# A graph convolution and a graph attention layer in fp32: one weight kept on chip, four reloaded through two buffers, norms moved, operands laid out anew

## The chip, the core and the metric

The kernel runs on one core of a Trainium2 chip. The core has five engines with a queue of instructions each: TensorE (PE in the profile, with PEld for its weight loads), VectorE (DVE), ScalarE (ACT), GpSimd (POOL) and SyncE (SP), which here issues every DMA. Engines wait for each other by semaphores; each works through its own queue in order. The metric is the device time of one execution in microseconds (us), as the median of several runs. Beside it there is one profiled execution, from which all durations here come.

## What is computed

The input is 128 graphs of 128 nodes with 512 features each, in fp32, and one adjacency matrix of 128x128. Two layers follow each other, both with a layer norm and a ReLU ahead and a residual addition behind:

```python
# layer 0: graph convolution
h = maximum(layernorm(x), 0)
norm_adj = adj * rsqrt(deg)[:, None] * rsqrt(deg)[None, :]
x = x + norm_adj @ (h @ weight) + bias
# layer 1: attention with 8 heads of 64, masked by adj
h = maximum(layernorm(x), 0)
q, k, v = h @ Wq + bq, h @ Wk + bk, h @ Wv + bv
scores = q @ k.T / 8 + (1 - adj) * -1e9
x = x + (softmax(scores) @ v) @ Wo + bo
```

All weights are 512x512. So each graph passes through five projections (W for the convolution, Q, K, V and the output), and the mixing by the adjacency matrix, the scores, the softmax and its product with v lie between them.

## The kernel before

**Groups and blocks.** Four graphs make a group, so there are 32 groups (`NG`). The main loop runs over t from 0 to 32, and a turn of it has five blocks, W, Q, K, V and Y, one for each projection. W(t) works on group t+1, Q, K and V on group t, Y on group t-1. A block has seven steps, W0 to W6 for instance, and each step a second part (W0b). `block` goes through the steps; at each it first calls what a dictionary called `plan` holds for this place, and then the step of the projection (`Projection.step` for the part without a letter, `rest` for b). `at(t, place, f, ...)` puts a call into the plan. This fixes the order of the instructions on every engine by hand; no scheduler moves them. SyncE has no steps of its own: a DMA is issued as soon as those before it in the queue are issued and its own semaphores allow.

**One projection.** A projection multiplies 512x512 by 512x512 blocks by the Winograd form of Strassen's method: seven products P1, P5, P2, P6, P3, P7, P4 of 256x256 blocks instead of eight, and three of these (P5 with P3, P2, P4) again in seven products of 128x128. The left operand (activations) and the right one (weights) are first combined: sums and differences of blocks, kept beside the blocks themselves. A full operand has 40 slots of 128 columns (128x5120 fp32, 2.6 MB). Left operands are combined for every group, by L367 to L370 (256-blocks) and by nine instructions of L78 (128-blocks), mostly on POOL. Weights are combined once, stored to DRAM with their sums and reloaded for every group.

PE's products go to PSUM banks: bank_a for the 256-products, bank_d (two banks) for P5 and P3, bank_b for P2, bank_c for P4. Step 1 writes bank_d with P5; VectorE adds it to the result in two parts (`read_seven`, L432), the second at step 2b. Step 2 writes the first phase of bank_b; step 4 its second phase and then P3 into bank_d again, for which VectorE must have left bank_d. P4's phases go to bank_c at step 6 and, as a `tail`, in steps 1 and 2 of the next block; K alone does them in its own steps 4 to 6 (`whole`).

**Weights.** Three buffers `w_buf` take the five weights in turn (order 0, q, k, v, o). `prefetch` issues a reload in four parts of ten slots, each at a step of the block that is running (steps 3 to 6; in Y all four at step 3). `keep_w` stores a combined weight to DRAM once.

**Norms.** `Norm.scale` does, for two graphs of a half group, BATCH_NORM_STATS (L320) and its aggregate (L321) of each, then `ve` (L322: variance plus epsilon) on VectorE, then the power (L323) and two small products (L325) on POOL. `ln1` calls it for the first layer at Q1b and Q3b, `ln2` for the second at V0 and V1b. ScalarE then writes the normalised graph (L336). Of the first layer it goes through PE for the mixing (`gcn_mix`, L604), of the second through PE for a transpose (`transpose_h`, L668), and ScalarE copies the result into the slots of the left operand (`blocks_of`).

**Attention.** At V0 stand `attend` of the group before (softmax times v, L797), the `scores` (L730, evicted by L737 or L734) and the combinations of the output operand. `row_max` (L749), `exponentials` (L757) and `softmax_end` (L764, L765) are spread over V, Y, and the next W and Q. For the transpose of the softmax, `split_att` (L770, L771) writes two planes of 16 bits to DRAM and `turn_att` (L774) reads them back by a transposing DMA.

Of the kernel before, what the change touches and what calls it, by code (L numbers as in the profile page):

```python
# [11 lines left out]
ALU = mybir.AluOpType  # L12
# [14 lines left out]
A11, A12, S1, A22, S2, S3, S4 = range(7)  # L27
# [16 lines left out]

LEFT_AT = {A11: 0, A12: 4, S1: 11, A22: 18, S2: 25, S3: 29, S4: 33}
RIGHT_AT = {W11: 0, T1: 4, W21: 11, T2: 18, W22: 22, T3: 29, T4: 33}
SLOTS = 40


# [20 lines left out]

def twice(t, at, n):

    return t[:, at[0] + n : at[1] + n + 1 : at[1] - at[0], :]


def combine_one(engine, t, at, step):
    out, x, y, minus = step
    engine.tensor_tensor(twice(t, at, out), twice(t, at, x), twice(t, at, y), ALU.subtract if minus else ALU.add)  # L78


def combine_within(engine, t, at, steps):
    for step in steps:
        combine_one(engine, t, at, step)


@with_exitstack
def kernel(
# [67 lines left out]


    w_sb, w_dram = {}, {}

    w_buf = [wp.tile([P, SLOTS, P], F32, tag=f"w{i}", name=f"w{i}") for i in range(3)]

    class Weight:
# [6 lines left out]
        def slot(self, k, n):  # L168
            return self.t[:, RIGHT_AT[k] + n, :]

# [9 lines left out]
    def keep_w(name):  # L180
        w_dram[name] = dp.tile([P, SLOTS, P], F32, tag=f"w_{name}", name=f"wd_{name}")
        nc.sync.dma_start(w_dram[name], w_sb[name].t)

    reloads = []

    def next_buffer():
        reloads.append(None)
        return w_buf[(len(reloads) - 1) % 3]

    def reload_w(name, part, parts):  # L190

        if part == 0:
            w_sb[name] = Weight(next_buffer())
        some = slice(part * SLOTS // parts, (part + 1) * SLOTS // parts)
        nc.sync.dma_start(w_sb[name].t[:, some, :], w_dram[name][:, some, :])

# [79 lines left out]
    def combine_inner(name, engine, steps=range(9)):  # L276
        for k in steps:
            pair, step = INNER[k]
            combine_one(engine, w_sb[name].t, tuple(RIGHT_AT[b] for b in pair), step)

# [25 lines left out]
    class Norm:  # L306


        def __init__(self, src, name):
# [5 lines left out]
            self.nb = sp.tile([P, 2], F32, tag="nb", name=f"nb_{name}")  # L315

        def scale(self, js):
            c = slice(js[0], js[-1] + 1)
            for j in js:
                nc.vector.bn_stats(self.st[:, j, :], self.src[:, j, :])  # L320
                nc.vector.bn_aggr(self.mv[:, j, :], self.st[:, j, :])  # L321
            nc.vector.tensor_scalar(self.ve[:, c], self.mv[:, c, 1], EPS, None, ALU.add)  # L322
            nc.gpsimd.tensor_tensor(self.rs[:, c], self.ve[:, c], mhalf[:, c], ALU.pow)  # L323
            for j in js:
                nc.gpsimd.tensor_scalar(  # L325
                    self.nb[:, j : j + 1], self.mv[:, j, 0:1], self.rs[:, j : j + 1], -1.0, ALU.mult, ALU.mult
                )
# [18 lines left out]
    class Operands:  # L346
# [6 lines left out]
        def slot(self, i, n):  # L353
            return self.t[:, LEFT_AT[i] + n, :]

        def blocks_of(self, b):

            half, j = divmod(b, 2)
            x, y = ((A11, A12), (S1, A22))[half]
            step = LEFT_AT[y] - LEFT_AT[x]  # L360
            t = self.t[:, LEFT_AT[x] : LEFT_AT[x] + 2 * step, :].rearrange("p (y s) n -> p y s n", y=2)
            return t[:, :, j : j + 3 : 2, :]

        def combine(self, engine, inner=True, then=None, within=None):

            t, then, within = self.blocks, then or engine, within or engine
            engine.tensor_tensor(t(S3), t(A11), t(S1), ALU.subtract)  # L367
            engine.tensor_tensor(t(S1), t(S1), t(A22), ALU.add)
            then.tensor_tensor(t(S2), t(S1), t(A11), ALU.subtract)
            then.tensor_tensor(t(S4), t(A12), t(S2), ALU.subtract)  # L370
            if inner:
                combine_within(within, self.t, (LEFT_AT[S1], LEFT_AT[S4]), FIRST_LEFT)
                combine_within(within, self.t, (LEFT_AT[A12], LEFT_AT[A22]), WINOGRAD_LEFT)

# [212 lines left out]

    def ln1(g, half, js=(0, 1)):
        if (g, half) not in scale1:
            scale1[g, half] = Norm(xts[g, half], f"1_{g}_{half}")  # L590
        scale1[g, half].scale(js)

# [4 lines left out]
    def gcn_mix(g, b):  # L597
        if b == 0:

            op_a[g] = op_att if g == 1 else op_mix  # L600
        h = hs.pop((g, b))
        pa = small_bank(f"pa_{g}_{b}")
        for c in range(NC):
            nc.tensor.matmul(pa[:, c * P : (c + 1) * P], h[:, c * P : (c + 1) * P], ant, start=True, stop=True)  # L604
        src = pa.rearrange("p (y c n) -> p y c n", y=2, c=2)
        if g == 1 and b < 2:
            nc.vector.tensor_copy(op_a[g].blocks_of(b), src)
        else:
            nc.scalar.copy(op_a[g].blocks_of(b), src)  # L609
# [42 lines left out]

    def ln2(g, half, js=(0, 1)):
        if (g, half) not in scale2:
            scale2[g, half] = Norm(xts[g, half], f"2_{g}_{half}")
        scale2[g, half].scale(js)

# [4 lines left out]
    def transpose_h(g, b):  # L662
        if b == 0:
            op_h[g] = op_norm
        h2 = hs.pop((g, b))
        pt = small_bank(f"pt_{g}_{b}")
        for c in range(NC):
            nc.tensor.transpose(pt[:, c * P : (c + 1) * P], h2[:, c * P : (c + 1) * P], ident)  # L668
        nc.scalar.copy(op_h[g].blocks_of(b), pt.rearrange("p (y c n) -> p y c n", y=2, c=2))

# [114 lines left out]
    def attend(g, b):  # L785
        if g not in op_o:

            op_o[g] = op_mix if g == NG - 1 else op_att
        aT = att_of(g, b if g == NG - 1 else b - 1)
        if b == 2 or b == 3:  # L790
            po = small_bank(f"po_{g}_{b}")
        else:
            po = bank["b" if b == 0 else f"a{1 - turn[0]}"]
        for c in range(NC):
            for p in range(2):
                h = 2 * c + p
                nc.tensor.matmul(  # L797
                    po[p * HD : (p + 1) * HD, c * P : (c + 1) * P],
                    vs[g][:, b, h * HD : (h + 1) * HD],
                    aT[:, p * NC + c, :],  # L800
                    start=True,
                    stop=True,
                )
        nc.scalar.copy(op_o[g].blocks_of(b), po.rearrange("p (y c n) -> p y c n", y=2, c=2))

# [19 lines left out]
    for t in range(-1, NG + 1):  # L825
# [3 lines left out]
        if 0 <= t - 1 < NG - 1:  # L829
            g = t - 1  # L830
            for place, first, f, *args in (
                ("W1", "W1", turn_att, 0),
                ("W1b", "W4b", split_att, 1),
# [4 lines left out]
                ("W6", "Q2", exponentials, 3, H // 2, H),  # L838
                ("Q0", "Q0", turn_att, 1),
                ("Q0b", "Q2b", softmax_end, 3),  # L840
                ("Q3b", "Q4b", split_att, 2),
                ("Q5b", "Q6b", split_att, 3),
                ("K1", "K1", turn_att, 2),
                ("K3", "K3", turn_att, 3),
            ):
# [18 lines left out]
        elif 1 <= t + 1 < NG and t >= 0:  # L864
            g = t + 1

            at(t, "V0", ln2, g, 0)
            at(t, "V1b", ln2, g, 1)
            at(t, "V5b", norm_h, g, 0)
            at(t, "V6", norm_h, g, 1)  # L870
# [12 lines left out]
        if 3 <= t + 2 < NG:  # L883
            at(t, "W3" if t > 1 else "W0", load_x, t + 2, (0,))
            at(t, "W6" if t > 1 else "W0", load_x, t + 2, (1,))
        if 2 <= t + 2 < NG:
            g = t + 2
            at(t, "Q0b" if t == 0 else "Q1b", ln1, g, 0)
            at(t, "Q3b", ln1, g, 1)
# [7 lines left out]
        if 0 <= t < NG:  # L897
# [16 lines left out]
            else:  # L914
                if t > 0:
                    at(t, "V4b", row_max, g, 1)
                    at(t, "Y1", exponentials, g, 1, 0, H // 2)
# [31 lines left out]


    uses = ["v", "o"]
    for t in range(2, NG + 1):
        uses += ["0"] if t + 1 < NG else []
        uses += ["q", "k", "v"] if t < NG else []
        uses += ["o" if t < NG else "o last"]

    def prefetch(part):
        if not uses:
            return
        if uses[0] != "o last":  # L960
            reload_w(uses[0], part, 4)
        elif part == 0:
            load_w("o last", wo, next_buffer())
        if part == 3:
            uses.pop(0)

    def block(t, kind, g, dense_of):
        dense = dense_of(g) if 0 <= g < NG else None
        for n in range(7):
            for place, part in ((f"{kind}{n}", 0), (f"{kind}{n}b", 1), (f"{kind}{n}c", 2)):  # L970
                for f, *args in plan.get((t, place), ()):
                    f(*args)
                if dense is not None and part < len(dense[n]):
                    if n > 2 and part == 0 and t > 0 and (t, kind) != (1, "W"):
                        for m in ((n - 3,) if kind != "Y" else range(4) if n == 3 else ()):
                            prefetch(m)
                    dense[n][part]()

    def prologue():
# [68 lines left out]
        at(0, "V0", combine_inner, "k", nc.gpsimd)  # L1048
        at(0, "V2", keep_w, "k")
        at(1, "Q2b", combine_w, "o", nc.gpsimd)  # L1050
# [6 lines left out]
    with tc.manual_schedule(  # L1057
# [7 lines left out]
    ):  # L1065
        prologue()

        for t in range(NG + 1):
# [52 lines left out]
```

## Time and profile before

| | |
|---|---|
| median of 3 runs | 2340.53 us (2339.39 to 2341.41) |
| the profiled execution, its own time | 2341.13 us |
| its span from the first to the last instruction | 2339.3 us |
| mean granted TensorE clock | 0.997 |
| period of one group in the middle of the run | 71.5 us |
| bytes moved by DMA | 617.35 MB, mean 264 GB/s, queue busy for 82.7% of 16 engines |

How to read the lines: a row of a timeline has the start in us from the span's start, the duration in us, the engine, the line of the kernel, the operation, the tile that it writes and those that it reads with shapes, and how many equal instructions are merged in the row. In brackets stands how long the engine was idle before it and what released it. A row of a waits view has who waited, for whom, the total in us, how often, and the longest. PE's matmuls are pipelined: a 128x128 one takes about 0.275 us from start to end, and the next starts 0.11 us after it.

### The profile page before, as it was taken

How to read it: one execution, taken by the hardware profiler on the slowest of the kernel's cores; microseconds unless marked ns; L12 is line 12 of the kernel's file. 1: busy time of each engine (PE TensorE's matmuls, PEld its weight loads, DVE VectorE, ACT ScalarE, POOL GpSimd, SP SyncE). 2: the span in 40 equal slices, each digit the busy share in tenths (PEclk: the TensorE clock that was granted, in tenths of full speed). 3: DMA queues.
4: the chain of work that ended last, by engine and by line, in shares of the span. 5: the costliest groups of instructions: out<-in, count | busy, mean ns of one | idle time of the engine just before them, and what ended most of it. 6: DMA issues, size and time to landing. Idle time of an engine off the chain costs nothing.

```text
span 2339.3 us, 51019 instructions
## 1 busy us (share of the span) xinstructions
PE 2291.9 (98%) x18359; PEld 2149.0 (92%) x18359; DVE 1881.7 (80%) x4832; ACT 1347.5 (58%) x3553; POOL 1862.7 (80%) x1927
## 2 busy tenths in 40 slices
PE   9889999999999999999999999999999999999999
PEld 8789999999999999999999999999999999999988
DVE  7767888788888878887888888788878888887876
ACT  3545656556656556565566565565655665655564
POOL 6888788777888777887778887778877788877664
PEclk9999999999999999999999999999999999999999
DMA  5488887898888998889988789987899888898773
GB/s 199 172 285 289 247 264 262 284 300 262 269 262 258 298 291 250 266 261 284 300 254 279 259 258 296 286 261 266 259 284 300 257 271 264 257 295 299 232 263 114
DMA packets 408189, 617.35 MB, mean 264 GB/s; under 512 B 273792, under 2 KB 281088, under 8 KB 407296
## 3 DMA queue, kind: packets, MB, share of 16 engines
q1 hardware_dynamic: 407936, 614.09, 82.7%
q8 instruction: 146, 2.39, 0.4%
q14 instruction: 107, 0.88, 0.1%
HBM read 437.33 MB, written 111.67 MB: 235 GB/s over the span
## 4 chain that ended last, share of the span: by engine, by line
PE 77%; DVE 14%; issue 2%; POOL 0%; ACT 0%; DVEq 0%
PE bank_a L391 27%; PE bank_d L391 17%; PE bank_c L391 10%; PE bank_b L391 7%; PE pa L604 4%; DVE st L320 3%; DVE v L432 3%; DVE q L432 3%; PE po L797 3%; DVE att L737 2%; PE pt L668 2%; PE bank_d L730 2%; DVE xt L432 1%; PE pss L730 1%; PE bank_b L797 1%
## 5 line engine op out<-in xcount | busy, mean ns | idle before, releaser
L757 ACT ACTIVATE att<-att,nmx 128x128 f32<-128x128 f32 x1024 | 396.0, 389 | 0.6 <-DVE nmx L749 0.5
L391 PE MATMUL bank_a<-op_h,w 128*128 128x256 f32 x1536 | 363.3, 379 | 0.0
L391 PEld LDWEIGHTS bank_a<-op_h,w 128*128 128x128 f32 x1536 | 277.6, 190 | 30.0
L765 POOL TENSOR_TENSOR att<-att,rsm 128x1024 f32<-128x1024 f32 x128 | 242.9, 1898 | 73.2 <-DVE rsm L764 69.9
L432 DVE TENSOR_TENSOR xt<-xt,bank_d 128x512 f32<-128x512 f32 x732 | 269.0, 416 | 27.0 <-PE bank_d L391 9.0
L336 ACT ACTIVATE h<-xt,nb,rs 128x512 f32<-128x512 f32 x254 | 204.0, 816 | 72.9 <-POOL nb L325 71.2
L691 ACT ACTIVATE q<-bank_a,bqk 128x256 f32<-128x256 f32 x192 | 80.5, 470 | 277.4 <-PE bank_a L391 277.4
L770 ACT COPY att<-att 128x2048 uint16<-128x2048 uint16 x124 | 235.5, 1899 | 8.1 <-POOL att L765 8.1
L391 PE MATMUL bank_d<-op_h,w 128*128 128x128 f32 (+1 forms) x1768 | 225.5, 279 | 11.1 <-DVE q L432 7.9
L391 PEld LDWEIGHTS bank_d<-op_h,w 128*128 128x128 f32 x1768 | 210.6, 192 | 17.2 <-issue 12.5
L78 POOL TENSOR_TENSOR op_o<-op_o 128x256 f32<-128x256 f32 x297 | 209.6, 729 | 10.0
L78 POOL TENSOR_TENSOR op_h<-op_h 128x256 f32<-128x256 f32 x279 | 197.0, 730 | 12.8 <-DVE op_h L370 3.2
L78 POOL TENSOR_TENSOR op_a<-op_a 128x256 f32<-128x256 f32 x270 | 190.9, 731 | 14.4 <-DVE op_a L370 5.1
L367 POOL TENSOR_TENSOR op_a<-op_a 128x512 f32<-128x512 f32 x29 | 37.0, 1275 | 203.6 <-ACT op_a L609 203.6
L757 ACT ACTIVATION_READ_ACCUMULATOR att<-att,nmx 128x1 f32 x1024 | 193.0, 188 | 0.0
L442 DVE TENSOR_TENSOR xt<-bank_a,xt 128x512 f32<-128x512 f32 x252 | 167.4, 685 | 18.5 <-PE bank_a L391 10.9
L391 PE MATMUL bank_a<-w,op_o 128*128 128x256 f32 x768 | 181.7, 379 | 0.0
L391 PE MATMUL bank_a<-w,op_h 128*128 128x256 f32 x744 | 179.1, 384 | 0.0
L391 PE MATMUL bank_a<-w,op_a 128*128 128x256 f32 x744 | 176.2, 380 | 1.2 <-DVE xt L442 1.2
L320 DVE BATCH_NORM_STATS2 st<-xt 128x6 f32<-128x512 f32 x256 | 172.3, 673 | 3.4 <-DMA xt<-in_x_dram 3.4
L705 ACT COPY v<-bank_a 128x512 f32<-128x512 f32 x96 | 56.3, 586 | 189.8 <-PE bank_a L391 145.4
L323 POOL TENSOR_TENSOR rs<-ve,mhalf 128x2 f32<-128x2 f32 (+1 forms) x129 | 92.1, 714 | 92.0 <-DVE ve L322 91.8
(178 smaller groups left out, 6091.9 us busy)
## 6 DMA issues: line engine op xcount, KB each, us to landing
w<-wd_v SPq DMA_DIRECT2D x124, 640.0 KB, 6.5
w<-wd_o SPq DMA_DIRECT2D x124, 640.0 KB, 6.9
w<-wd_q SPq DMA_DIRECT2D x120, 640.0 KB, 4.4
w<-wd_k SPq DMA_DIRECT2D x120, 640.0 KB, 8.0
w<-wd SPq DMA_DIRECT2D x116, 640.0 KB, 11.1
planes<-att SPq DMA_DIRECT2D x124, 512.0 KB, 4.4
xt<-in_x_dram SPq DMA_DIRECT2D x63, 512.0 KB, 6.7
out_dram<-xt SPq DMA_DIRECT2D x62, 512.0 KB, 3.9
```

The source lines that it names most:

```text
L78: engine.tensor_tensor(twice(t, at, out), twice(t, at, x), twice(t, at, y), ALU.subtract if minus else ALU.add)
L320: nc.vector.bn_stats(self.st[:, j, :], self.src[:, j, :])
L323: nc.gpsimd.tensor_tensor(self.rs[:, c], self.ve[:, c], mhalf[:, c], ALU.pow)
L336: nc.scalar.activation(h, src[:, j, :], AF.Relu, bias=nb[:, j : j + 1], scale=rs[:, j : j + 1])
L391: nc.tensor.matmul(out, lhsT, rhs, start=start, stop=True, skip_group_check=True)
L432: nc.vector.tensor_tensor(dst, dst, src, f)
L442: nc.vector.tensor_tensor(t, src.rearrange("p (r f) -> p r f", r=2), t, ALU.add)
L604: nc.tensor.matmul(pa[:, c * P : (c + 1) * P], h[:, c * P : (c + 1) * P], ant, start=True, stop=True)
L757: nc.scalar.activation(att[:, h, :], att[:, h, :], AF.Exp, bias=nmx[:, h : h + 1], scale=1.0, accum_out=sm[:, h : h + 1])
L765: nc.gpsimd.tensor_tensor(att, att, rsm.unsqueeze(2).to_broadcast([P, H, P]), ALU.mult)
L770: nc.scalar.copy(planes, halves)
L797: nc.tensor.matmul(po[p * HD : (p + 1) * HD, c * P : (c + 1) * P], vs[g][:, b, h * HD : (h + 1) * HD], aT[:, p * NC + c, :], start=True, s ...
```

## The change

Five things change; the order of PE's instructions does not.

- Weights: "k" stays in the third buffer for the whole run, and is neither stored nor reloaded. The other four ("0", q, v, o) share the first two buffers in turn, and are reloaded in four parts of 11, 11, 11 and 7 slots, cut where the products cut them (`PARTS`), at places listed by hand in `reloads_of`.
- Layer norm: the statistics of one graph (`statistics`) are a call of their own, so that `ln1` can do the first graph of a half at Q0b and the second, with the scale of both, at Q1b.
- The second norm's `ln2` goes from V0 and V1b to K0b and K3b; the first normalisation behind it from V5b to V5, and the second `row_max` of V from V4b to V3b.
- The transposing reads `turn_att` go from W1, Q0, K1, K3 to Q0, Q2, K0, K2; one x load goes from W6 to W5.
- The left operand's slots: the four plain blocks lie side by side (0, 4, 8, 12), the sums of 128-blocks behind them, so that `blocks_of` is one access with one stride. `twice` finds the slots by `slot_of`.

```diff
-LEFT_AT = {A11: 0, A12: 4, S1: 11, A22: 18, S2: 25, S3: 29, S4: 33}
+LEFT_AT = {A11: 0, A12: 4, S1: 8, A22: 12, S2: 16, S3: 20, S4: 24}
+LEFT_MORE = {A12: 28, A22: 31, S1: 34, S4: 37}
 RIGHT_AT = {W11: 0, T1: 4, W21: 11, T2: 18, W22: 22, T3: 29, T4: 33}
+PARTS = ((0, 11), (22, 33), (11, 22), (33, 40))
+def slot_of(left, k, n):
+    if not left:
+        return RIGHT_AT[k] + n
+    return LEFT_AT[k] + n if n < 4 else LEFT_MORE[k] + n - 4
...
         def blocks_of(self, b):
             half, j = divmod(b, 2)
-            x, y = ((A11, A12), (S1, A22))[half]
...
+            first = LEFT_AT[S1 if half else A11]
+            return self.t[:, first + j : first + 8 : 2, :]
...
+        def statistics(self, j):
+            nc.vector.bn_stats(self.st[:, j, :], self.src[:, j, :])
+            nc.vector.bn_aggr(self.mv[:, j, :], self.st[:, j, :])
         def scale(self, js):
             c = slice(js[0], js[-1] + 1)
-            for j in js:
-                nc.vector.bn_stats(self.st[:, j, :], self.src[:, j, :])
-                nc.vector.bn_aggr(self.mv[:, j, :], self.st[:, j, :])
             nc.vector.tensor_scalar(self.ve[:, c], self.mv[:, c, 1], EPS, None, ALU.add)
...
+        for j in js:
+            scale1[g, half].statistics(j)
+        if ready is None or ready:
+            scale1[g, half].scale(ready or js)
...
-                ("W1", "W1", turn_att, 0),
+                ("Q0", "W1", turn_att, 0),
...
-                ("Q0", "Q0", turn_att, 1),
+                ("Q2", "Q0", turn_att, 1),
...
-                ("K1", "K1", turn_att, 2),
-                ("K3", "K3", turn_att, 3),
+                ("K0", "K1", turn_att, 2),
+                ("K2", "K3", turn_att, 3),
...
-            at(t, "V0", ln2, g, 0)
-            at(t, "V1b", ln2, g, 1)
-            at(t, "V5b", norm_h, g, 0)
+            at(t, "K0b", ln2, g, 0)
+            at(t, "K3b", ln2, g, 1)
+            at(t, "V5", norm_h, g, 0)
...
-            at(t, "W6" if t > 1 else "W0", load_x, t + 2, (1,))
+            at(t, "W5" if t > 1 else "W0", load_x, t + 2, (1,))
...
-            at(t, "Q0b" if t == 0 else "Q1b", ln1, g, 0)
+            at(t, "Q0b", ln1, g, 0, (0,), ())
+            at(t, "Q1b", ln1, g, 0, (1,), (0, 1))
...
-                    at(t, "V4b", row_max, g, 1)
+                    at(t, "V3b", row_max, g, 1)
...
+    uses, reading = [], [-1]
+    for t in range(1, NG + 1):
         uses += ["0"] if t + 1 < NG else []
-        uses += ["q", "k", "v"] if t < NG else []
+        uses += ["q", "v"] if t < NG else []
         uses += ["o" if t < NG else "o last"]
+    def reload_w(n, part):
...
+        if part == 0:
+            w_sb[name] = Weight(w_buf[n % 2])
+        some = slice(*PARTS[part])
+        nc.sync.dma_start(w_sb[name].t[:, some, :], w_dram[name][:, some, :])
+    def reloads_of(t):
+        when = {
+            "W": ((t, "W6"), (t, "Q4"), (t, "Q1"), (t, "K3")),
+            "Q": ((t, "K4"), (t, "K6"), (t, "V0"), (t, "V1")),
+            "V": ((t, "V3"), (t, "Y0"), (t, "Y1"), (t, "Y3")),
+            "Y": ((t, "Y5"), (t + 1, "W0"), (t + 1, "W0"), (t + 1, "W3" if t + 1 < NG - 1 else "Q5")),
+        }
...
+        for kind in "WQVY":
...
+            reading[0] += 1
+            for part, place in enumerate(when[kind]):
+                at(*place, reload_w, reading[0] + 2, part)
...
-        at(0, "V2", keep_w, "k")
```

In `reloads_of`, the entry under "W" tells where the buffer that W reads is filled again, for V; that under "Q" the same for Y, under "V" for the next W, under "Y" for the next Q.

## The prediction

> **What bounds the kernel now.** I read the page's first part, then TensorE's own waits, then one steady group in order of time. The page:
>
> ```profile
> span 2339.3 us, 51019 instructions
> PE 2291.9 (98%) x18359; PEld 2149.0 (92%) x18359; DVE 1881.7 (80%) x4832; ACT 1347.5 (58%) x3553; POOL 1862.7 (80%) x1927
> ...
> w<-wd_k SPq DMA_DIRECT2D x120, 640.0 KB, 8.0
> ```
>
> PE is busy for 98%, so only its pauses can be won, and its matmuls are not touched: their order is the same in both kernels. The waits of PE alone say which pauses come back in every group (columns: total us, times, longest):
>
> ```profile
> PE bank_d L391 <- DVE v L432: 10.8, 28, 0.4
> PE bank_d L391 <- DVE q L432: 7.9, 29, 0.4
> ```
>
> Everything else in that view happens once or twice, at the ends. No matmul waits for a weight. In the group from 1000 to 1071.5 us (the period is 71.5 us) PE's two pauses stand here:
>
> ```profile
> 1024.67 0.61 PE L391 MATMUL bank_b<-w,op_h 128*128 128x128 f32 x4
> 1025.65 1.80 PE L391 MATMUL bank_d<-w,op_h 128*128 128x128 f32 x14 [0.38 <-DVE v L432]
> ...
> 1061.61 0.61 PE L391 MATMUL bank_b<-op_h,w 128*128 128x128 f32 x4
> 1062.48 1.80 PE L391 MATMUL bank_d<-op_h,w 128*128 128x128 f32 x14 [0.27 <-DVE q L432]
> ```
>
> Four 128x128 matmuls go out in 0.447 us, so bank_d was due at 1025.12 and came 0.54 late; its 14 matmuls then take 1.80 instead of 1.73. One V4 costs 0.61 us, one Q4 0.43 + 0.07 = 0.50. What makes VectorE late in V is here:
>
> ```profile
> 1020.02 0.68 DVE L320 BATCH_NORM_STATS2 st<-xt 128x6 f32<-128x512 f32 x1
> ...
> 1021.75 0.47 DVE L322 TENSOR_SCALAR ve<-mv 128x2 f32<-128x2 f32 x1
> ...
> 1023.59 0.86 DVE L432 TENSOR_TENSOR v<-v,bank_b 128x256 f32<-128x256 f32 x2
> 1024.37 1.14 DVE L432 TENSOR_TENSOR v<-v,bank_d 128x128 f32<-128x128 f32 x4
> ```
>
> VectorE does not rest from 1020.02 until it frees bank_d at 1025.51; the norm's 2.1 us stand in front. The trace holds its own control: the last group's V has no norm in it, and there PE goes
>
> ```profile
> 2298.01 0.61 PE L391 MATMUL bank_b<-w,op_h 128*128 128x128 f32 x4
> 2298.56 1.80 PE L391 MATMUL bank_d<-w,op_h 128*128 128x128 f32 x14
> ```
>
> that is 0.10 + 0.07 = 0.18 us, no more. The last Q (no norm either) shows the same 0.18 (2267.13 to 2267.68, then 1.80). This residue stays: bank_b's matmuls end late enough that VectorE's six additions (1.93 us) reach bank_d's release only 0.03 us before PE wants it.
>
> **The change, part by part.**
>
> *Second norm out of V (ln2 from V0, V1b to K0b, K3b).* V1b loses 2.1 us of VectorE. Its reads then start when bank_b is ready: PE's phase ends 1023.10, plus 1.93 is 1025.06, 0.05 before need. I take the control: 0.61 falls to 0.18, 0.43 x 30 groups = 12.9 us. The half at V0 lay in idle time (1.22 us stood before the first score eviction) and gains nothing there. row_max moving from V4b to V3b stays in front of the same six reads; ScalarE's normalisation at V5 instead of V5b fills a 1.4 us gap in which ScalarE waits for VectorE anyhow. Both: 0. On POOL, `rs` and `nb` of the norm (L323, L325: 0.7 + 0.5 us) move too: the first half's to a stretch of 7.28 us in which POOL waits for op_a, the second half's behind op_a's combinations at 1015.6, where the first half's stood; op_o's combinations behind them start when they did. 0.
>
> *First norm split (Q0b one element, Q1b the other).* In Q, VectorE stood idle 0.77 us before the bank_c read at 1057.40. One element's statistics (0.69 + 0.18, next instruction 0.82 later) fit in it to within 0.05. The rest at Q1b ends near 1058.95 instead of 1059.74; the bank_d and bank_c reads follow by 1059.81, and bank_b is ready at 1060.08, so again 1060.08 + 1.93 = 1062.01 against a need at 1062.05. 0.50 falls to 0.18: 0.32 x 29 = 9.4 us. Cover: the x load must have landed by 1056.5; before it landed at 1054.30 and was wanted at 1057.93.
>
> *What the norm costs in K.* K0b: VectorE idles 2.19 us before the bank_c read at 1000.52 and POOL is idle until 1003.64; 1.81 us fit. Cost 0. K3b is tight:
>
> ```profile
> 1006.27 0.61 DVE L432 TENSOR_TENSOR k<-k,bank_b 128x128 f32<-128x128 f32 x2 [0.24 <-PE bank_b L391]
> 1007.93 0.29 DVE L432 TENSOR_TENSOR k<-k,bank_c 128x128 f32<-128x128 f32 x1 [1.05 <-ACT k L694]
> ...
> 1008.52 0.61 PE L391 MATMUL bank_c<-op_h,w 128*128 128x128 f32 x4
> ```
>
> The norm now stands in front of these rows: VectorE's last bank_d addition starts at 1005.616, the next instruction 0.33 later, at 1005.95. It takes 1.81 (its length in Q, POOL idle: 1057.93 to 1059.74); behind it wait two bank_b additions (next start 0.53 later) and the bank_c addition (0.29), which K5's first bank_c matmul waits for. It frees bank_c at 1008.59; PE wants it at 1008.52. The nearest row for such a near miss is W's bank_c behind VectorE: released 0.008 us late it loses 0.153, so 0.065 + 0.145 = 0.21 us. Later steps of K keep their distance (bank_c's last phase is freed 0.1 before PE needs it). Bounds: 0 (VectorE a tenth faster) and 1.35 (below). 0.21 x 30 = 6.3 us.
>
> *Where row and rule part.* The norm's last instruction, `ve`, takes 0.17 us when POOL is idle (66 cases), but 0.46 to 0.50 in V under POOL's L370: in all of these it ended 0.023 us after POOL's instruction did. The Trainium skill (SBUF — State Buffer, "Who interferes with whom") speaks against the move: VectorE's tensor_scalar in its two-port mode and a GpSimd instruction share a port pair, and the one that issues first keeps it for its whole instruction. At K3b POOL combines op_a:
>
> ```profile
> 1006.35 1.27 POOL L369 TENSOR_TENSOR op_a<-op_a 128x512 f32<-128x512 f32 x1
> 1007.69 1.27 POOL L370 TENSOR_TENSOR op_a<-op_a 128x512 f32<-128x512 f32 x1
> ```
>
> `ve` is due at 1005.947 + 1.735 (from the first statistics to `ve`, as in Q) = 1007.68: over the steady groups 4 to 25 ns before L370 starts, inside a 67 ns gap. By the V row (0.3 held) K5 loses 0.51 and the sum is 7 us won. By the rule with `ve` first it is not held: 16 us won. With POOL first it is held till 1008.98, 1.14 us more: K5 loses 1.35. I take "first by start", but the stamps need not be the moment of asking: at 75.49 us VectorE's L296 took 1.30 us though the POOL instruction that held it started 22 ns after it.
>
> *K resident, four weights in two buffers.* Removes 120 DMAs of 640 KB (78.6 MB) and one 2.6 MB store: 617 to 536 MB. PE never waited for weights, so 0 is won. What it adds are waits on SyncE: each part must wait until PE has left the part it overwrites, in the buffer that was read one use before the last. SyncE issues in order, so behind such a wait stand the planes stores, the turns, the output stores and the x loads, and ScalarE, PE and VectorE behind those. Cover, at 1.6 us per 640 KB (spacing of landings): V's first part is asked for at W6 and read 36 us later; o's by 1005 and read at 1030; "0" lands by about 1040, read from 1043 on; q's first part is issued behind the planes store at 1040.8, lands by 1046, read at 1055; its middle parts at 1045, landing near 1051, read at 1059. Each has 3 us or more. If that cover goes, PE waits for the difference. The two turns moved from W1 and Q0 to Q0 and Q2, the others one step earlier, stand behind fewer bytes: before, the second turn held SyncE for 9.1 us behind K's reloads. Landings of 1008.69 and 1010.67 (wanted at 1011.24 and 1012.1) come earlier; the two real PE waits on them (2.0 us, first group) may shrink: 0 to 2 won, 0 taken. The x load stays at W3, behind the output store that VectorE releases at 1048.5, but now has q's two middle parts (1.4 MB, 3.5 us) before it instead of a turn (2.1 us); from the output store's first landing at 1047.5 I add 3.5 for q, 1.2 for planes, 1.3 for the second store, 1.3 for x: landing 1054.8, wanted 1056.5.
>
> *Other layout of left operands.* Copies keep 512 elements in runs of 128, combinations keep 128x256 at other strides: 0, bounds -1 to +1 us.
>
> **Sum.** -12.9 - 9.4 + 6.3 = -16.0. The profiled execution took 2341.13 (span 2339.3 + 1.8 around it), 0.6 above the median: 2325.1 profiled, 2324.5 as median.
>
> **Rivals.**
> *POOL gets the port pair first at K3b (slower).* 28 groups have L370 there. Cost 1.35 x 28 + 0.4 = 38.2 against 22.3 won: +15.9, 2356.5. It decides once `ve` is held over 0.55 us on average (0.21 + 0.55 = 0.76, the gain of V and Q). For it: the 22 ns case, the rule; against: `ve` starts first in all groups. If groups differ: 2330 to 2350.
> *The pause only moves, or x lands late.* VectorE has 0.3 us to spare at Q1b; an x load 2.5 us later than I reckon gives Q its pause back and more: 9 us lost, 2334 to 2342. For it: 3.5 us of weights before it; against: 1.7 us of slack.
> *K3b costs nothing.* 22 won, 2318.
>
> **How the numbers follow.** My case (2319 to 2331) 0.60, K3b free 0.06, groups differing 0.08, late or moved 0.08, POOL first 0.18. A kernel like this is told from no change at 0.2%, 4.7 us. Faster: 0.60 + 0.06 + half of each middle case = 0.74; same 0.07; slower 0.19. The range runs from K3b free to the upper end of the mixed cases, 2317 to 2350, and leaves out most of POOL first.
>
> **What would show it.** Period 70.95 instead of 71.5; PE's waits on v and q gone or under 2 us; a new PE wait bank_c <- DVE k of some 2 us; `ve` at K3b 0.17. If wrong: `ve` of 1.3 us there and PE waiting some 1.1 us per group for k; or a wait of DVE st on the x load; or PE rows waiting for DMA w.

## The result and the profile after

The changed kernel takes 2331.15 us (median of 7 runs, 2329.11 to 2334.98), against 2339.74 us for the kernel before in the same comparison (2336.09 to 2342.24). The ratio is 0.9965, 95% interval 0.9954 to 0.9977: 8.6 us faster, and the interval leaves out 1. The forecast was 2324.5, 15 to 16 us faster: direction right, gain about half. The profiled execution of the changed kernel took 2329.11, its span is 2327.3, so between the two profiles there are 12.0 us; the sums below are made between those two spans.

All line numbers below are those of the kernel whose profile is shown. In the changed kernel the additions into a tile are L428 (L432 before), matmuls L387 (L391), statistics L313 and `ve` L318 (L320, L322), the last combination of op_a L364 (L370).

The page's first part and its row for the statistics of a norm (busy us, mean ns of one | idle before them and what ended it):

```profile
span 2327.3 us, 50893 instructions
PE 2300.2 (99%) x18359; PEld 2155.6 (93%) x18359; DVE 1869.4 (80%) x4832; ACT 1344.8 (58%) x3553; POOL 1861.7 (80%) x1927
...
L313 DVE BATCH_NORM_STATS2 st<-xt 128x6 f32<-128x512 f32 x256 | 173.2, 676 | 24.8 <-DMA xt<-in_x_dram 24.8
```

The same row in the kernel before:

```profile
L320 DVE BATCH_NORM_STATS2 st<-xt 128x6 f32<-128x512 f32 x256 | 172.3, 673 | 3.4 <-DMA xt<-in_x_dram 3.4
```

The work of PE and VectorE is the same in number. New is the last figure: VectorE's statistics wait 24.8 us for x, where they waited 3.4 us before. TensorE's own waits (total us, times, longest):

```profile
PE bank_c L387 <- DVE xt L428: 5.6, 11, 1.3
PE pa L604 <- ACT h L332: 4.1, 1, 4.1
...
PE bank_b L387 <- DVE q L428: 0.6, 1, 0.6
PE bank_d L387 <- issue: 0.3, 1, 0.3
PE bank_c L387 <- DVE k L428: 0.3, 1, 0.3
```

The two groups of waits in every group of the run, on v and on q, are gone, as forecast. A wait on `xt` has come in their place. The view puts 5.6 us down to it (1.3 of them once, at the start, as in the kernel before). Reckoned from the starts of the matmuls, with the short pauses and the lengthened rows that the view leaves out, it is 8.8 us in the steady groups, as is seen below. The wait on k that was forecast stands in the view only once, for 0.3 us: in the steady groups it is too short for the view. PE and VectorE in V of one group, in order of time (start, duration):

```profile
1374.65 0.61 PE L387 MATMUL bank_b<-w,op_h 128*128 128x128 f32 x4
1375.16 1.80 PE L387 MATMUL bank_d<-w,op_h 128*128 128x128 f32 x14
```

```profile
1372.30 0.42 DVE L428 TENSOR_TENSOR v<-v,bank_d 128x256 f32<-128x256 f32 x1 [1.09 <-PE bank_d L387]
1373.12 0.88 DVE L428 TENSOR_TENSOR v<-v,bank_b 128x256 f32<-128x256 f32 x2 [0.40 <-PE bank_b L387]
1373.91 1.14 DVE L428 TENSOR_TENSOR v<-v,bank_d 128x128 f32<-128x128 f32 x4
```

Four 128x128 matmuls go out in 0.447 us, so bank_d came 0.06 us late instead of 0.54. VectorE now waits for PE before these reads (1.09 and 0.40 us), where it was busy without a rest before. And K3b, VectorE above, POOL below:

```profile
1354.68 1.14 DVE L428 TENSOR_TENSOR k<-k,bank_d 128x128 f32<-128x128 f32 x4
1355.74 0.69 DVE L313 BATCH_NORM_STATS2 st<-xt 128x6 f32<-128x512 f32 x1
...
1357.47 0.17 DVE L318 TENSOR_SCALAR ve<-mv 128x2 f32<-128x2 f32 x1
1357.55 0.60 DVE L428 TENSOR_TENSOR k<-k,bank_b 128x128 f32<-128x128 f32 x2
1358.07 0.28 DVE L428 TENSOR_TENSOR k<-k,bank_c 128x128 f32<-128x128 f32 x1
```

```profile
1356.14 1.27 POOL L363 TENSOR_TENSOR op_a<-op_a 128x512 f32<-128x512 f32 x1
1357.49 1.28 POOL L364 TENSOR_TENSOR op_a<-op_a 128x512 f32<-128x512 f32 x1
```

`ve` starts 12 to 29 ns before POOL's L364 in the steady groups and takes 0.169 to 0.171 us in all of them. It is not held. The part of the norm that stayed costs what was forecast: PE's row for K5 is now

```profile
1356.75 1.73 PE L387 MATMUL bank_d<-op_h,w 128*128 128x128 f32 x14
1358.40 0.71 PE L387 MATMUL bank_c<-op_h,w 128*128 128x128 f32 x4
```

In the kernel before, the row at 1008.52, 0.61 us long, stood behind this one:

```profile
1006.96 1.73 PE L391 MATMUL bank_d<-op_h,w 128*128 128x128 f32 x14
```

So K5 starts 0.09 us late and its first row is 0.10 longer.

Where the rest went is seen best in the group with the longest wait. VectorE, then PE:

```profile
1262.88 0.20 DVE L768 RECIPROCAL rsm<-sm 128x8 f32<-128x8 f32 x1
1264.91 0.69 DVE L313 BATCH_NORM_STATS2 st<-xt 128x6 f32<-128x512 f32 x1 [1.84 <-DMA xt<-in_x_dram]
1265.64 0.18 DVE L314 BATCH_NORM_AGGREGATE mv<-st 128x2 f32<-128x6 f32 x1
1265.74 0.57 DVE L428 TENSOR_TENSOR xt<-xt,bank_c 128x128 f32<-128x128 f32 x2
```

```profile
1263.64 1.73 PE L387 MATMUL bank_d<-op_h,w 128*128 128x128 f32 x14
1266.37 0.49 PE L387 MATMUL bank_c<-w,op_a 128*128 128x128 f32 x2 [1.00 <-DVE xt L428]
```

The first norm's first element (Q0b) waits for its x load 1.84 us. Behind it on VectorE stand the two bank_c additions of the mix, and PE's last two bank_c matmuls in Q1 wait for these: 1.16 us lost here. In 22 of the 28 steady groups x is late, by 0.3 to 1.84 us.

Summed over 28 steady groups, as the gap from the last matmul of one phase to the first of the next, less the usual spacing (for K5 and Q1 with the lengthening of the row behind it; that of V4 and Q4, 0.07 us, is in both kernels):

| pause of PE | before, us | after, us | forecast of the difference | measured |
|---|---|---|---|---|
| V4, bank_d | 15.4 | 1.7 | -12.9 | -13.7 |
| Q4, bank_d | 11.7 | 4.1 | -9.4 | -7.6 |
| K5, bank_c | 0 | 5.7 | +6.3 | +5.7 |
| Q1, bank_c (x late) | 0 | 8.8 | 0 | +8.8 |
| up to V's first scores in group 2 | | | 0 to -2 | -4.5 (228.2 to 223.8) |

These make -11.3 of the 12.0 us between the spans; the rest are smaller waits, most of them in the last groups. The last line is in large part the scatter of the start: PE's first wait for op_o, 6.1 us in the profile before and 3.2 after, is 5.8 to 6.0 in three other profiles with the new reloads and 3.2 in one with the old.

### The profile page after: what moved, and what is told of

It reads as the page before. It is cut to its first block, busy times and chain, and to the rows that moved or that the text cites. A ratio compares the mean times of both kernels' runs of the same rounds, so it can differ in the third digit from the quotient of the medians.

```text
span 2327.3 us, 50893 instructions
## 1 busy us (share of the span) xinstructions
PE 2300.2 (99%) x18359; PEld 2155.6 (93%) x18359; DVE 1869.4 (80%) x4832; ACT 1344.8 (58%) x3553; POOL 1861.7 (80%) x1927
## 4 chain that ended last, share of the span: by engine, by line
PE 82%; DMA 5%; DVE 5%; issue 1%; POOL 0%; SPq 0%; ACT 0%; DVEq 0%; ACTq 0%
PE bank_a L387 30%; PE bank_d L387 18%; PE bank_b L387 9%; PE bank_c L387 9%; DMA xt<-in_x_dram 5%; PE pa L604 4%; PE bank_d L734 3%; PE po L801 3%; PE pt L672 2%; DVE xt L428 2%; PE pss L734 1%; DVE xt L438 1%; PE bank_b L801 1%; PE bank_a L801 1%; PE bank_b L734 1%
## 5 line engine op out<-in xcount | busy, mean ns | idle before, releaser
L387 PE MATMUL bank_a<-op_h,w 128*128 128x256 f32 x1536 | 364.6, 380 | 0.0
L387 PEld LDWEIGHTS bank_a<-op_h,w 128*128 128x128 f32 x1536 | 278.6, 191 | 30.3
L428 DVE TENSOR_TENSOR xt<-xt,bank_d 128x512 f32<-128x512 f32 x732 | 269.1, 416 | 25.9 <-PE bank_d L387 9.0
L387 PE MATMUL bank_d<-op_h,w 128*128 128x128 f32 (+1 forms) x1768 | 225.5, 279 | 3.9 <-POOL op_h L90 3.1
L387 PEld LDWEIGHTS bank_d<-op_h,w 128*128 128x128 f32 x1768 | 210.7, 192 | 9.1 <-issue 4.0
L313 DVE BATCH_NORM_STATS2 st<-xt 128x6 f32<-128x512 f32 x256 | 173.2, 676 | 24.8 <-DMA xt<-in_x_dram 24.8
L387 PE MATMUL bank_a<-w,op_o 128*128 128x256 f32 x768 | 181.7, 379 | 0.0
L387 PE MATMUL bank_a<-w,op_h 128*128 128x256 f32 x744 | 179.1, 384 | 0.0
L387 PE MATMUL bank_a<-w,op_a 128*128 128x256 f32 x744 | 176.8, 381 | 0.2 <-DVE xt L438 0.2
L741 DVE SCALAR_TENSOR_TENSOR att<-bank_d,msk 128x512 f32<-128x512 f32 x128 | 82.5, 686 | 104.8 <-PE bank_d L734 96.2
L753 DVE TENSOR_REDUCE nmx<-att 128x8 f32<-128x1024 f32 x128 | 155.0, 1211 | 0.0
```

Source lines behind the costliest of these rows:

```text
L387: nc.tensor.matmul(out, lhsT, rhs, start=start, stop=True, skip_group_check=True)
L428: nc.vector.tensor_tensor(dst, dst, src, f)
L753: nc.vector.tensor_reduce(nmx, att_of(g, b), AX.X, ALU.max, negate=True)
```

## The experiments

My theory after the result: the two norm moves do what was forecast, and the loss is one thing, the x load landing behind q's middle weight parts. The rivals: V and Q's pauses cannot both go (the pause only moves), the weights in two buffers cost something of their own, or the left operands' layout moves the times. The first four kernels were compared with the kernel before at 2341.25 us (2339.01 to 2342.74), the last four with 2341.91 (2336.72 to 2344.09). "Period" is the mean time from one group's V to the next over the 27 middle groups: 71.508 us before, 71.255 after.

**x ahead of q's parts.** The changed kernel; q's two middle parts are issued behind the x loads.

```
-            "Y": ((t, "Y5"), (t + 1, "W0"), (t + 1, "W0"), (t + 1, "W3" if t + 1 < NG - 1 else "Q5")),
+            "Y": ((t, "Y5"), (t + 1, "W5"), (t + 1, "W3"), (t + 1, "W5"))
+            if t + 1 < NG - 1
+            else ((t, "Y5"), (t + 1, "W0"), (t + 1, "W0"), (t + 1, "Q5")),
```

> The changed kernel with q's middle reload parts moved behind the x load (second part read at Q2 asked for at W3 after the x load, the others at W5). Theory (x waits behind q's two middle parts, 1.4 MB, in SyncE's queue): x lands some 3 us earlier, VectorE's waits for x (22 of 28 steady groups) go, PE's waits at the tail of W in Q1 (6.9 + 1.9 us over 28 groups) go, and Q4's residue falls from 0.15 to 0.06 in the mean (2.5 us): 11 us under the changed kernel, about 2320, ratio to before 0.992. Rival (the rate of the DMA queue alone makes x late, wherever the parts stand): VectorE still waits for x, 2331, ratio 0.9965. Rival (q's parts now come too late themselves): PE rows waiting for a DMA of w in Q2 or Q4, 2335 or more.

Measured: 2318.04 us (2317.27 to 2319.67), ratio 0.9902, interval 0.9889 to 0.9916. The period is 70.834. The page's row of the statistics and the queue's order in one group:

```profile
L313 DVE BATCH_NORM_STATS2 st<-xt 128x6 f32<-128x512 f32 x256 | 171.7, 671 | 3.3 <-DMA xt<-in_x_dram 3.3
```

```profile
1389.73 0.38 SPq L819 DMA_DIRECT2D out_dram<-xt  x1
1390.20 0.42 SPq L160 DMA_DIRECT2D xt<-in_x_dram  x1
1390.71 0.83 SPq L971 DMA_DIRECT2D w<-wd_q  x1
1393.03 0.37 SPq L160 DMA_DIRECT2D xt<-in_x_dram  x1
1393.45 0.93 SPq L971 DMA_DIRECT2D w<-wd_q  x2
```

x lands at 1394.50, 4.3 us after its issue; in the changed kernel's group shown further below it took 8.2. With this one edit the waits for x are gone after the start, the Q4 pause is 0.06 us in every steady group, and no matmul waits for a part of q. 13 us come back by the medians, 11.8 between the two profiles' spans. The bytes are the same. So the loss was the order of the queue.

**First norm whole again.** The changed kernel, with the first norm of half 0 not split.

```
-            at(t, "Q0b", ln1, g, 0, (0,), ())
-            at(t, "Q1b", ln1, g, 0, (1,), (0, 1))
+            at(t, "Q0b" if t == 0 else "Q1b", ln1, g, 0)
```

> The changed kernel with the first norm of a half done whole at Q1b again (both graphs' statistics there). Theory (the split at Q0b wants x 1.4 us earlier than it lands): no wait of VectorE for x, so 8.8 us of PE's waits in Q1 go; but Q4's pause is back at 0.43 instead of 0.15 per group (8 us lost), and the start's first norm is earlier by 2 to 3 us: 2327 to 2331, about as the changed kernel. Rival (the split is worth the whole 9.4 us and the late x costs nothing): 2340, as before.

Measured: 2328.16 us (2327.45 to 2329.84), ratio 0.9946, 0.9932 to 0.9959; period 71.219. Q's pause is back at 0.38 us per group (10.7 us over 28), and x, wanted later, is late in four groups only, by 0.2 to 0.9 us, for which no matmul waits. So the split, with x where the change left it, brings nothing: it loses more by the wait for x than it wins at Q4 (3.0 us by the medians, 1.7 by the spans).

**Norms alone.** The kernel before with only the two norm moves (second norm at K0b and K3b, norm_h at V5, row_max at V3b, first norm split); weights, turns, loads and layout as before.

```
-            at(t, "V0", ln2, g, 0)
-            at(t, "V1b", ln2, g, 1)
-            at(t, "V5b", norm_h, g, 0)
+            at(t, "K0b", ln2, g, 0)
+            at(t, "K3b", ln2, g, 1)
+            at(t, "V5", norm_h, g, 0)
...
-            at(t, "Q0b" if t == 0 else "Q1b", ln1, g, 0)
+            at(t, "Q0b", ln1, g, 0, (0,), ())
+            at(t, "Q1b", ln1, g, 0, (1,), (0, 1))
```

> The kernel before with the norm parts of the change alone: first norm split by graph, second norm in K, normalisation at V5, row_max at V3b; three buffers, five reloads, places of the turns and layout as before. Theory (the gain is the norms' and the late x comes with the new order of reloads): in the queue of before x lands at 54.3 of the reference group, wanted at 56.5, so no wait for it; V wins 15 us, Q 10, K costs 5.5, the start costs up to 3: 2320 to 2323, ratio 0.992, faster than the changed kernel. Rival (the lighter DMA queue carries the gain, or x is late here too): 2331 or more, ratio 0.9965 or above.

Measured: 2325.16 us (2323.67 to 2327.36), ratio 0.9934, 0.9921 to 0.9948; period 70.924. x is wanted just as early here, but the old order of the queue brings it in time in all groups but one. That is the forecast's sum (-16.0) at -16.1, though 2 us above what I expected of this run, and the whole change is 6 us slower than this part of it.

**`ve` later at K3b.** The changed kernel, with one aggregate of the second norm's half 1 computed a second time before `ve` (the same values, 0.18 us more on VectorE), so that `ve` comes behind the start of POOL's L364.

```
+        for _ in range(again):
+            norm = scale2[g, half]
+            nc.vector.bn_aggr(norm.mv[:, 1, :], norm.st[:, 1, :])
...
-            at(t, "K3b", ln2, g, 1)
+            at(t, "K3b", ln2, g, 1, (0, 1), None, 1)
```

> The changed kernel with one statistics aggregate repeated in K3b ahead of the norm's last VectorE instruction ve (same values written again), so that ve starts 0.1 to 0.2 us later, after POOL's fourth op_a combination has begun instead of 12 to 29 ns before it. Theory (the engine that starts first keeps the port pair for its whole instruction): ve is held until that combination ends, 1.1 to 1.3 us instead of 0.17; K5's bank_c comes 1.2 us late instead of 0.19: 28 groups x 1.15 = 32 us more, about 2363, slower than before by 1%. Rival (ve is not held, the 12 to 29 ns decide nothing): only the 0.1 to 0.2 us themselves, 2334 to 2337.

Measured: 2359.78 us (2358.77 to 2360.63), ratio 1.0080, 1.0066 to 1.0093: slower than the kernel before. VectorE and POOL at K3b, and PE's wait:

```profile
1013.77 0.18 DVE L661 BATCH_NORM_AGGREGATE mv<-st 128x2 f32<-128x6 f32 x1
1013.99 1.08 DVE L318 TENSOR_SCALAR ve<-mv 128x2 f32<-128x2 f32 x1
1014.99 0.59 DVE L428 TENSOR_TENSOR k<-k,bank_b 128x128 f32<-128x128 f32 x2
```

```profile
1013.78 1.27 POOL L364 TENSOR_TENSOR op_a<-op_a 128x512 f32<-128x512 f32 x1
```

```profile
PE bank_c L387 <- DVE k L428: 31.5, 29, 1.5
```

`ve` starts 0.20 us after L364 here, 0.18 to 0.20 in all 28 groups, and ends 0.02 to 0.03 after it: 1.1 us in place of 0.17. K5 starts 1.23 us late and its first row is 0.10 longer, 1.34 us per group; summed as in the table it is 36.8 us, against 5.7. Q1's pause falls from 8.8 to 5.6, since x is less late where everything else is later. An instruction of 0.18 us cost 28 us because of what it let past.

**Second norm alone.** The kernel before with only the second norm's move (the first three pairs of lines of the norms' diff above, and row_max at V3b).

> The kernel before with the second norm's move alone (K0b, K3b; norm_h at V5, row_max at V3b); the first norm whole at Q1b, weights, turns, loads and layout as before. My theory: V's pause falls from 0.55 to about 0.1 us per group (12 to 14 us won), K5 gains 0.19 per group (5.5 us lost), Q keeps its 0.42: 2341 - 7 to 9 = 2332 to 2334. Rival: the norms only help together (Q's split alone brings what the kernel with both norms won, 16 us), and this kernel stays within 3 us of the kernel before, at 2338 to 2344.

Measured: 2333.81 us (2331.2 to 2334.6), ratio 0.9966, 0.9952 to 0.9979; period 71.256. V's pause is 0.107 us, Q's stays at 0.427, K5's two are 0.088 and 0.101. So the second norm is worth 8 us alone and the first a further 8 on top of it (-8.1 and -8.0, each uncertain by some 3 us).

**Weights, turns and layout alone.** The changed kernel with both norms put back at the places of the kernel before.

```
-            at(t, "K0b", ln2, g, 0)
-            at(t, "K3b", ln2, g, 1)
-            at(t, "V5", norm_h, g, 0)
+            at(t, "V0", ln2, g, 0)
+            at(t, "V1b", ln2, g, 1)
+            at(t, "V5b", norm_h, g, 0)
...
-            at(t, "Q0b", ln1, g, 0, (0,), ())
-            at(t, "Q1b", ln1, g, 0, (1,), (0, 1))
+            at(t, "Q0b" if t == 0 else "Q1b", ln1, g, 0)
```

> The changed kernel with its norms put back (second norm at V0 and V1b, norm_h at V5b, row_max at V4b, first norm whole at Q1b): what is left of the change is the weights in two buffers, the turns and the layout. My theory from the other runs: V's and Q's pauses as before; the first groups win 4 us (the turns stand behind fewer bytes); the first norm whole at Q1b waits for x only in a few groups: 2341 - 3 to 5 = 2336 to 2338. Rival of the prediction as it stood: these parts bring nothing, 2340 to 2342, and the 7 us between norms alone and norms with x ahead belong to a joint effect.

Measured: 2336.83 us (2333.99 to 2340.43), ratio 0.9983, 0.9974 to 0.9991; period 71.434. It does bring something, 5 us by the medians. In the trace 2.6 us of it lie before the second group, and the pauses are a little shorter in every group (V 0.47 for 0.55, Q 0.385 for 0.43). Whether the weights or the turns bring it was not run. The parts make 8.1 + 8.0 + 5.1 = 21.2 us; together they made 8.6. The x load, which either part alone leaves in time in all groups but one, accounts for the 12.6 us between, as far as these differences carry, each being uncertain by 2 to 3 us: putting it ahead gave back 13.1.

**Old layout of left operands.** The first experiment's kernel (x ahead), with the blocks of a left operand seven slots apart again and the evictions in 2 x 2 runs.

```
-LEFT_AT = {A11: 0, A12: 4, S1: 8, A22: 12, S2: 16, S3: 20, S4: 24}
-LEFT_MORE = {A12: 28, A22: 31, S1: 34, S4: 37}
+LEFT_AT = {A11: 0, A12: 4, S1: 11, A22: 18, S2: 25, S3: 29, S4: 33}
+LEFT_MORE = {A12: 8, S1: 15, A22: 22, S4: 37}
```

> The kernel with the x load ahead (2318.0), with the old layout of left operands put back (blocks seven slots apart, evictions as 2 x 2 runs); everything else as there. It asks where the residue of V and Q goes, which is 0.106 us in the kernel with the norms alone and 0.06 in the kernels with the weights' part. If the layout does it: residues of 0.106 again, period 70.92 in place of 70.83, about 2320.5. If the lighter traffic does it: 0.06, 70.83, 2318.

Measured: 2317.49 us (2314.59 to 2323.46), ratio 0.9903, 0.9888 to 0.9918; period 70.848, against 0.9902 and 70.834 with the new layout. Residues 0.06. The layout is worth nothing that these runs can show.

**Half 1's norm in three places.** The first experiment's kernel (x ahead), with the statistics of the second norm's half 1 split between K1b and K3b and `ve`, `rs` and the scale at V0. It asks whether the last new pause, K5, is only a matter of how much stands at K3b.

```
-            at(t, "K3b", ln2, g, 1)
+            at(t, "K1b", ln2, g, 1, (0,), ())
+            at(t, "K3b", ln2, g, 1, (1,), ())
+            at(t, "V0", ln2, g, 1, (), (0, 1))
```

> This kernel is the one with the x load ahead, with one thing more: the second norm's half 1 no longer runs as a whole at K3b; its first element's statistics go to K1b, its second's to K3b, and ve, rs and the scale to V0. My theory: what K3b puts in front of the bank_b and bank_c additions falls from 1.81 to about 0.9 us, so bank_c is free some 0.85 us before TensorE wants it, and the pauses of 0.08 + 0.10 us at K5 in every group go: 0.18 x 29 = 5.2 us, 2318.0 to about 2313; ve, now at V0, may be held by POOL there (0.46 to 0.50 us in the kernel before) and costs nothing, since VectorE waits there for the first score eviction. Rival one: K1b has no room and the pause only moves to K3's banks: 2317 to 2321. Rival two: POOL's scale is late for norm_h in V5, and V or Y pauses: over 2320.

Measured: 2313.17 us (2311.84 to 2317.05), ratio 0.9882, 0.9868 to 0.9896; period 70.666. VectorE at K3b:

```profile
1066.83 0.69 DVE L313 BATCH_NORM_STATS2 st<-xt 128x6 f32<-128x512 f32 x1
1067.55 0.18 DVE L314 BATCH_NORM_AGGREGATE mv<-st 128x2 f32<-128x6 f32 x1
1067.65 0.57 DVE L428 TENSOR_TENSOR k<-k,bank_b 128x128 f32<-128x128 f32 x2
1068.81 0.29 DVE L428 TENSOR_TENSOR k<-k,bank_c 128x128 f32<-128x128 f32 x1 [0.59 <-ACT k L698]
```

VectorE waits again before the bank_c addition, and K5's pauses are gone from the steady groups (0.17 us of the period). `ve`, at V0, takes 0.34 to 0.37 us there and nobody waits for it. This is the lowest median: 28.7 us below the kernel before in its comparison. Against the x-ahead kernel the two intervals overlap, and the two profiled spans are alike (2315.3 and 2315.5), since this one's start took 4.5 us longer; what tells them apart is the period, 70.666 against 70.834, of one profile each.

## Why the prediction was right and wrong

**What bounds the kernel, right.** PE's pauses were all there was to win, and the two in V and Q went when VectorE's norm left the place in front of the reads.

**V4 and Q4, right in kind, somewhat small in size.** I took the last groups' residue of 0.18 us as the floor. With the norms alone it is 0.106 + 0.07, as in that control; in the changed kernel V's is 0.06 + 0.07, and Q's too where x is in time. The 0.045 between is not the layout (residues 0.06 with the old one). In the records, a semaphore instruction with VectorE's wait stands ahead of bank_d's first weight load. With the new parts of the weights it also carries the wait for one of these parts, and is there early; with the old ones it carries VectorE's alone, and begins only when bank_b's last weights are loaded. I read that in the two traces; no kernel here tests it. (Two slips in my sums change nothing: 1023.10 + 1.93 is 1025.03, and 0.32 x 29 is 9.3.)

**K5, right.** 0.21 us per group was forecast for a bank_c freed 0.065 us late; 0.19 was measured, with bank_c freed 0.04 late, and splitting the norm takes it away.

**`ve` against POOL's combination, right, with little to spare.** The rule of the Trainium skill (SBUF — State Buffer, "Who interferes with whom"), that the instruction that issues first keeps the port pair, fits what `ve` did at K3b. 12 to 29 ns ahead of L364 it took 0.17 us in every group, and so it did in the five other kernels that have it there (11 to 39 ns ahead, 140 cases); 0.18 to 0.20 us behind it, it was held to L364's end. The rival's bound for that case, K5 at 1.35 us, was measured at 1.34, and its time, 2356.5, at 2359.8. The rule's other half is not seen: as the second of the two, L364 should have waited for the 0.14 us or more that `ve` still ran, but it took 1.272 to 1.287 us, against 1.271 to 1.280 in the kernel before.

The row at 75.49 us in the kernel before, where an instruction that started 22 ns ahead was held all the same, comes back in all ten traces (20 to 29 ns ahead, 1.29 to 1.30 us). It starts while VectorE's instruction ahead of it still runs, and that one ends 12 to 18 ns after the one ahead on POOL. At K3b both of these had ended before `ve` and L364 started. So if each instruction counts from the end of the one ahead of it, POOL was first in that row, and it fits the rule too. That is read from the stamps; no run tests it.

**The cover of the x load, wrong: this is the step that failed.** The first norm's split was costed on an x load landing at 1054.8 and wanted at 1056.5, 1.7 us of slack. Here is SyncE in one group of the changed kernel (VectorE wants x at 1406.12 there, which answers to 1056.5):

```profile
1393.55 0.39 SPq L819 DMA_DIRECT2D out_dram<-xt  x1
1394.03 1.30 SPq L971 DMA_DIRECT2D w<-wd_q  x2
1395.42 0.46 SPq L775 DMA_DIRECT2D planes<-att  x1
1398.04 0.39 SPq L819 DMA_DIRECT2D out_dram<-xt  x1
1398.52 1.04 SPq L160 DMA_DIRECT2D xt<-in_x_dram  x1
```

and the landings that the trace gives for these, beside those that I added up, moved by the same 349.6 us:

| transfer | forecast | landed | forecast step | measured step | median of 28 groups |
|---|---|---|---|---|---|
| first output store | 1397.1 | 1396.88 | | | |
| q's two middle parts | 1400.6 | 1403.00 | 3.5 | 6.1 | 5.51 (4.31 to 6.69) |
| planes | 1401.8 | 1404.30 | 1.2 | 1.3 | 1.39 |
| second output store | 1403.1 | 1405.46 | 1.3 | 1.2 | 1.26 |
| x | 1404.4 | 1406.75 | 1.3 | 1.3 | 1.29 |

The order in the queue was right, and so were all steps but one in the median (single ones of the last three run from 0.8 to 2.9). I gave q's two parts 1.75 us each, from the spacing at which 640 KB reloads land when they follow one another. Here the first of the two lands 3.59 us after the store ahead of it (median), the second 2.07 after the first. That is 2.0 us more than reckoned, against 1.7 of slack, and with a scatter of 2.4 us between groups, which goes with a pause that differs from group to group (a start 0 to 1.16 us late). The first part's issue follows the store's by 0.48 us, so no semaphore held it: it is the transfers themselves. Its packets of 5.5 KB took 0.33 us each, and the second part's 0.27 (medians over the groups). With x ahead the same two parts land 1.79 and 1.75 us after the x load ahead of each, as I had reckoned, with packets of 0.22. There their packets begin 3.2 and 3.6 us after the issue; here the first part's begin after 2.0, with little in the queue ahead of it. The changed kernel's other parts of this size go the same way: packets of 0.27 to 0.30 us where they begin within 2.1 us of the issue, of 0.22 to 0.23 where they begin later. So my spacing was that of parts that have waited in the queue. Why the others are slower stays open.

So the rival "x lands late" had the mechanism and nearly the size, and its sign, a wait of VectorE's statistics on the x load, is the one that came: it set 9 us lost for a load 2.5 us later; the load came 2.3 us later in this group, and the pause cost 8.8 us, with 2.4 more at Q4 (4.1 against 1.7 with x ahead). I gave it too small a chance, since I held 1.7 us against an estimate whose own error I had not bounded: I bounded the unknown costs on the engines from both sides, and this one, on the queue, from one. The time, 2331.15, lies between my own case (2319 to 2331) and that rival's (2334 to 2342), because the rest of my sum held.

**Weights in two buffers, zero: somewhat too little.** No matmul waits for weights, as forecast. With the norms put back, what is left of the change was 5 us faster than the kernel before, where I had allowed 0 to 2; 2.0 of it are the period over the 27 middle groups (71.434 against 71.508). The first groups may gain besides: V's scores of group 2 begin at 227.1 to 228.2 us in the three profiles with the old reloads, and at 222.0 to 227.6 in the seven with the new. The two waits on turns in the first group, 2.0 us, which were named as the upper end, are gone in the changed kernel, but one of the seven has 2.2 us of them. The ranges overlap, so how much of this the change brings is not shown.

## What to carry to other kernels

When work that needs a load is moved earlier and the loads' queue is reordered in the same change, add up the landings ahead of that load with a bound on each from both sides, and set the slack against the sum of the bounds: here 1.7 us of slack stood against a step that ran from 4.3 to 6.7 us, and either edit alone was harmless. If the order of issue is free, put the load that an engine waits for ahead of those with time to spare; that cost nothing here and was worth 12 to 13 us. And where a short VectorE instruction starts a few tens of nanoseconds ahead of a long GpSimd one, look at the order in every group and at what could delay it, since 0.18 us can become 1.1.

## What was not expected of the hardware

- 704 KB of weights behind an output store landed 2.5 to 5.0 us after it (28 groups), and a second part of the same size 1.7 to 2.6 us after the first, with no semaphore holding either. The same parts behind an x load, issued 3.2 to 3.6 us before their packets began, landed 1.75 and 1.79 us after it (medians).
- 11 to 39 ns ahead of POOL's instruction were enough for `ve` not to be held, in 168 cases of six kernels; 0.18 to 0.20 us behind, it was held in all 28. Held, it ended 0.02 to 0.03 us after POOL's instruction; not held, it took 0.168 to 0.171 us, while POOL's 1.27 us instruction was longer by no more than 0.02.
- A release that came a little late cost TensorE more than its lateness: VectorE's bank_c addition ends at 1358.35 (1358.07 + 0.28), 0.04 us after PE wanted the bank (1356.75 + 1.56, the spacing in the kernel before), and K5 lost 0.19, 0.10 of it as a longer first row of four matmuls (0.71 in place of 0.61).
